# Zero borders from a constant tile, pools that wait by tile, and a first group normalised by channel pairs, in a two-layer convolution kernel

## The chip, the cores and the metric

The kernel runs on one core of a Trainium2 chip. The metric is the device time of one execution in microseconds (us). The engines are called by their names: TensorE (PE in the profile; its weight loads are PEld), VectorE (DVE), ScalarE (ACT), GpSimd (POOL) and SyncE (SP). SP does nothing here but issue DMAs; ScalarE issues some too.

## What is computed

The input x is 32 images of 8 channels, 256 by 256, float32. Two layers follow, each with a residual:

```python
# layer 0
n = gn(x)                                   # GroupNorm: 4 groups of 2 channels
grid = n
for _ in range(15):                         # a coupled map lattice, depthwise 3x3
    mapped = 3.9 * grid * (1 - grid)
    grid = 0.85 * (0.7 * mapped + 0.3 * conv3x3(mapped, K_local)) + 0.15 * n
cml = clip(grid, 1e-4, 1 - 1e-4)
nca = sigmoid(conv1x1(relu(conv3x3(n, Wp) + bp), Wu) + bu)      # 128 hidden channels
g = sigmoid(conv1x1(relu(conv3x3(concat(n, cml, nca), Wg1) + bg1), Wg2) + bg2)
x = x + g * cml + (1 - g) * nca
# layer 1: quantised 3x3 convolution of gn(x), 8 to 8 channels, plus bias
x = x + conv_q(gn(x), weight) + bias
```

All 3x3 convolutions are padded by one zero on each side.

## The kernel before

Intermediate results lie in DRAM scratch tensors: `xp_s` (the normalised image split into a high part hi and a rest lo, with padded rows), `xq_s` (the normalised image with its columns in four phases, the lattice's input), `cm_s` (the lattice's result), `nc_s` (the nca result) and `y_s` (layer 0's result, one tensor an image). `xp_s`, `xq_s`, `cm_s` and `nc_s` exist 12 times and are used in turn; `y_s` exists 32 times. All but `xq_s` have 268 rows, of which rows 1 to 256 hold the image. Row 0 and rows 257 to 267 are the border and must be zero. They are written once at the start (L195 to L202): a tile `zt` of zeros, 258 wide, is the source of four DMAs for each of the 68 tensors, 272 in all, all issued by ScalarE. That code stands in the block of the pool `prep`, which also holds the raw weights; the pool is closed before layer 0 begins.

Layer 0 (from L257) opens its own pools in the space that `prep` gave back. A tile of such a pool that lies in reused space waits, before its first write, for the users of the space.

The work goes in 8 groups of 4 images (`GB`). Four generators give it:

- `normalise` (L288): for a job, an image and a half of its channels (two pairs of channels), `begin` loads each pair (`xr`, 512 KB, L300) and takes its statistics on VectorE (L305); `scale` and `end` get mean and 1/deviation with two small matmuls (L313, L324); then for each pair VectorE normalises (L331), ScalarE writes `xq` (L336), VectorE writes hi (L342), GpSimd writes lo (L343), and six DMAs on SP store them (L345, L352). `xr` has four buffers; `xq`, hi and lo have one each.
- `lattice` (L376): for each channel c of a group one unit of 15 steps over four images. Its input comes with `load(u)` (36 DMAs) in `d_a` and `d_b`. A step is 36 matmuls (L486) on three column tiles of two streams, and VectorE's work on them (L494, L499). Rows are exchanged between partitions by SBUF-to-SBUF DMAs on SP (`exchange`, L449 and L450). After each tile, `background(3)` issues up to three DMAs of the list `later`: the loads of the next unit and the stores of the last.
- `nca` (L553): the hidden layer (L563), its ReLU on ScalarE (L573) and the 1x1 convolution (L580), from row tiles `im` that SP loads from `xp_s` (L541).
- `gate`: the gate's convolution (L755) and the mix; it loads `nc_s`, `cm_s` and x on SP (`nb`, `cq`, `xb`).

TensorE's order is written by hand: `together` runs the lattice of group g and fills between its steps with nca of group g, gate of group g - 1 and normalise of group g + 1, by weights of time. The other engines' orders are the scheduler's, which may move an instruction ahead of others when its operands allow it. Each queue then runs in order.

The head is special: `prep(0, (0,))` normalises the first half (channels 0 to 3) of group 0's four images; then the lattice of group 0 begins, and the second half, `prep(0, (1,))`, runs as the first filling beside it, ahead of nca:

```python
for _ in prep(0, (0,)):
    pass
...
if g == 0:
    fill, t = chain(prep(0, (1,)), fill), t + 20.0
```

Layer 1 (from L879) reads `y_s` an image at a time, quantises and convolves; its pools wait by tile already.

Of the kernel before, what the change touches and what calls it, by code (L numbers as in the profile page):

```python
# [40 lines left out]
P = 128  # L41
C = 8
# [71 lines left out]
def kernel(  # L114
# [46 lines left out]
    rstd_y = cp.tile([P, B], F32, name="rstd_y")  # L161
    dev_y = cp.tile([P, B], F32, name="dev_y")


# [7 lines left out]
    with tc.tile_pool(name="prep", bufs=1) as pp, tc.tile_pool(name="prep2", bufs=2) as pp2:  # L172
# [20 lines left out]

        zt = pp.tile([P, PW], F32, name="zt")
        G.memset(zt, 0.0)  # L195
        for t, n, w in (
            *((t, 2 * C, PW) for t in xp_s), *((t, C, W) for t in (*cm_s, *nc_s, *y_s))
        ):
            nc.scalar.dma_start(dram_ap(t, 0, [[w, n], [1, w]]), zt[:n, :w])
            for i in range(0, 11, 5):  # L200
                m = min(5, 11 - i) * n
                nc.scalar.dma_start(dram_ap(t, (257 + i) * n * w, [[w, m], [1, w]]), zt[:m, :w])  # L202

# [53 lines left out]
    with ExitStack() as one:  # L257

        one.enter_context(tc.manual_schedule(engines={mybir.EngineType.PE}))
        pool = lambda name, bufs, **kw: one.enter_context(tc.tile_pool(name=name, bufs=bufs, **kw))  # L260
        xp, sp2, gp, bp2, st = pool("xp", 4), pool("sp2", 1), pool("gp", 3), pool("bp2", 2), pool("st", 2)
        imp, hp, wk, wk1, np_ = pool("imp", 3), pool("hp", 12), pool("wk", 2), pool("wk1", 1), pool("np", 1)
        ps_c, ps_a = pool("ps_c", 6, space=PSUM), pool("ps_a", 2, space=PSUM)
# [24 lines left out]
        def normalise(jobs):  # L288
# [3 lines left out]

            def begin(b, half):
                xrs = []
                mv = st.tile([P, 2, 2], F32, name="mv", tag="mv")
                stats = st.tile([P, 2, 2, 6], F32, name="stats", tag="stats")
                for i in range(2):
                    g = 2 * half + i
                    xr = xp.tile([P, 2, 2, W], F32, name="xr", tag="xr")
                    nc.sync.dma_start(  # L300
                        xr.rearrange("p c h w -> p (c h) w"),
                        dram_ap(x, (b * C + 2 * g) * H * W, [[W, P], [P * W, 4], [1, W]]),
                    )
                    for j in range(2):
                        V.bn_stats(stats[:, i, j, :], xr[:, j].rearrange("p h w -> p (h w)"))  # L305
                    V.bn_aggr(mv[:, i, :], stats[:, i].rearrange("p j s -> p (j s)"))
                    xrs.append(xr)
                return b, half, xrs, mv

            def scale(b, half, xrs, mv):  # L310
                gs = slice(2 * half, 2 * half + 2)
                pm = ps_c.tile([P, 512], F32, name="pm", tag="pt")
                T.matmul(pm[:, 0:2], avg, mv[:, :, 0], start=True, stop=True)  # L313
                m, rstd = mean_x[:, b, gs], rstd_x[:, b, gs]
                V.tensor_copy(m, pm[:, 0:2])
                e = st.tile([P, 2], F32, name="e", tag="e")
                V.tensor_tensor(e, mv[:, :, 0], m, ALU.subtract)
                V.tensor_tensor(e, e, e, ALU.mult)
                V.tensor_tensor(e, e, mv[:, :, 1], ALU.add)
                return e  # L320

            def end(b, half, xrs, e):
                pv = ps_c.tile([P, 512], F32, name="pv", tag="pt")
                T.matmul(pv[:, 0:2], avg, e, start=True, stop=True)  # L324
                rstd = rstd_x[:, b, 2 * half : 2 * half + 2]
                V.tensor_scalar(rstd, pv[:, 0:2], GN_EPS, None, ALU.add)
                G.tensor_tensor(rstd, rstd, mhalf[:, 0:2], ALU.pow)
                for i, xr in enumerate(xrs):
                    g = 2 * half + i
                    flat = xr.rearrange("p c h w -> p (c h w)")  # L330
# [12 lines left out]
                    G.tensor_tensor(inner(lo), xr, inner(hi).bitcast(F32), ALU.subtract)  # L343
                    for h in range(2):
                        nc.sync.dma_start(  # L345
                            dram_ap(
                                xq_s[b % NBUF], (2 * g * H + P * h) * W, [[W, P], [H * W, 2], [1, W]]
                            ),
                            xq[:, :, h].rearrange("p c q j -> p c (q j)"),
                        )  # L350
                        for j, src in enumerate((hi, lo)):
                            nc.sync.dma_start(  # L352
                                dram_ap(
                                    xp_s[b % NBUF],
                                    (1 + P * h) * ROW + (C * j + 2 * g) * PW,
                                    [[ROW, P], [PW, 2], [1, PW]],
                                ),
                                src.bitcast(F32)[:, :, h, :],
                            )
                    yield 1.0  # L360
                ready.add((b, half))

            ahead = None
            for job in [*jobs, None]:
                now = begin(*job) if job else None
                yield 1.0
                if ahead:
                    e = scale(*ahead)
                    yield 1.0
                    yield from end(*ahead[:3], e)  # L370
                ahead = now

        NG = B // GB
        ready = set()

        def lattice(g):  # L376


            def load(u):


                c, out, dmas = u % C, [], []
                assert all((u // C * GB + i, c // 4) in ready for i in range(GB))
                for s in range(2):
# [57 lines left out]
            def background(n):  # L442
                for _ in range(min(n, len(later))):
                    nc.sync.dma_start(*later.pop(0))

            def exchange(t, k):
# [106 lines left out]
        def nca(b):  # L553
# [80 lines left out]
            im = ahead  # L634
            if (b + 1, 0) in ready and (b + 1, 1) in ready:
                loaded[b + 1] = rows(b + 1, 0, 0)
# [217 lines left out]

        def prep(g, halves):
            return normalise([(b, half) for half in halves for b in range(g * GB, g * GB + GB)])

# [5 lines left out]
        T_NCA, T_GATE, T_PREP, T_LATTICE = 520.0, 340.0, 34.0, 8 * 45 * 1.97  # L863
        for _ in prep(0, (0,)):
            pass
        for g in range(NG):
            fill, t = images(nca, g), T_NCA
            if g:
                fill, t = both(fill, t, images(gate, g - 1), T_GATE), t + T_GATE
            if g + 1 < NG:  # L870
                fill, t = both(fill, t, prep(g + 1, (0, 1)), T_PREP), t + T_PREP
            if g == 0:
                fill, t = chain(prep(0, (1,)), fill), t + 20.0
            together(lattice(g), T_LATTICE, fill, t)
        for _ in images(gate, NG - 1):
            pass
# [113 lines left out]
```

## Time and profile before

| | us |
|---|---|
| three runs | 14463.03, 14468.11, 14472.73 |
| median | 14468.11 |
| the profiled execution | 14447.83 (span of the profile 14446.0) |
| busy: TensorE, VectorE, ScalarE, GpSimd | 13241.2, 8161.7, 4043.5, 2458.8 |
| first statistics of x on VectorE | at 118.3 |
| first dense lattice matmuls | at 217.8 |
| first hidden-layer matmul | at 311.7 |

The mean granted clock of TensorE is 0.959. In the profile's lines L12 is line 12 of the kernel, `out<-in` are the names of tiles or tensors, and "A <- B" in a list of waits says that A sat idle until B was done. The chain of waits follows the work that ended last back from the end, at each step to what released it. Times within a profile are us from its start.

### The profile page before, as it was taken

The numbers are of one execution on the slowest core, as the hardware profiler recorded it, in microseconds if no ns is written. First come the engines' busy times: TensorE is split into PE (matmuls) and PEld (weight loads), VectorE is DVE, ScalarE is ACT, GpSimd is POOL, SyncE is SP. The second block draws the span as 40 slices with busy tenths as digits, with TensorE's granted clock in tenths as the row PEclk, the third lists the DMA queues.
The fourth block names the chain that finished last, engine by engine and source line by source line (L and its number), as shares of the span: only waits on it lengthen the run. The fifth ranks groups of instructions, "written<-read, shape, count | busy, mean of one in ns | idle before, by whom it ended". The sixth has DMA issues, their size and how long they took to land.

```text
span 14446.0 us, 229162 instructions
## 1 busy us (share of the span) xinstructions
PE 13241.2 (92%) x81728; PEld 6420.6 (44%) x81728; DVE 8161.7 (56%) x16290; ACT 4043.5 (28%) x6274; POOL 2458.8 (17%) x4266
## 2 busy tenths in 40 slices
PE   2999999999999999999999999999999999999733
PEld 1554444444444444444444444444444444444211
DVE  3555555555555555555555555555555555555576
ACT  1333223232322232222223222322232222222122
POOL 1110111111111111111111111111111111112300
PEclk9999999999999999999999999999999999999866
DMA  5444444444444444444344434444444433333365
GB/s 149 93 101 93 92 99 105 101 95 104 105 97 101 106 98 98 101 100 111 88 101 105 108 91 102 103 108 94 97 104 108 95 84 80 86 75 79 114 195 176
DMA packets 2259557, 1496.71 MB, mean 104 GB/s; under 512 B 1061248, under 2 KB 2229504, under 8 KB 2258304
## 3 DMA queue, kind: packets, MB, share of 16 engines
q1 hardware_dynamic: 2176976, 1401.95, 41.1%
q10 hardware_dynamic: 81456, 80.12, 1.7%
q8 instruction: 663, 10.86, 0.3%
q14 instruction: 462, 3.78, 0.1%
HBM read 866.48 MB, written 478.69 MB: 93 GB/s over the span
## 4 chain that ended last, share of the span: by engine, by line
PE 76%; DVE 7%; DMA 7%; SPq 4%; issue 3%; ACT 1%; POOL 1%; ACTq 1%; POOLq 0%; DVEq 0%
PE pt L486 34%; PE ph L563 19%; PE pa L755 13%; PE acc L580 7%; DVE gt L494 2%; PE pg L721 1%; DMA im<-xp_s 1%; DMA out_dram<-ob 1%; SPq L941 1%; PE pt L934 1%; DVE m_b L499 1%; DMA yb<-y_s 1%; DMA m_a<-m_a 1%; DMA xb<-in_x_dram 1%; DMA xr<-in_x_dram 1%
## 5 line engine op out<-in xcount | busy, mean ns | idle before, releaser
L486 PE MATMUL pt<-m_a,lw 128*64 128x390 f32 x17280 | 5857.6, 497 | 160.4 <-DMA m_a<-m_a 121.4
L486 PE MATMUL pt<-m_b,lw 128*64 128x384 f32 x17280 | 5825.7, 492 | 23.0 <-DVE m_b L410 17.8
L573 ACT ACTIVATE h<-ph,bp_sb 128x512 f32<-128x512 f32 x4096 | 2584.7, 685 | 6258.0 <-PE ph L563 6187.8
L486 PEld LDWEIGHTS pt<-m_a,lw 128*64 128x64 f32 x17280 | 2312.1, 138 | 1824.9 <-issue 1670.8
L486 PEld LDWEIGHTS pt<-m_b,lw 128*64 128x64 f32 x17280 | 2316.1, 138 | 1601.4 <-issue 1465.6
L563 PE MATMUL ph<-im,wp_hi 48*128 48x512 f32 x12288 | 2713.5, 416 | 104.8 <-DMA im<-xp_s 54.4
L494 DVE SCALAR_TENSOR_TENSOR gt<-pt,d_b 128x390 f32<-128x390 f32 x2880 | 1610.6, 559 | 1828.2 <-PE pt L486 1824.9
L494 DVE SCALAR_TENSOR_TENSOR gt<-pt,d_a 128x384 f32<-128x384 f32 x2880 | 1584.9, 550 | 1826.9 <-PE pt L486 1826.5
L563 PE MATMUL ph<-im,wp_lo 48*128 48x512 f32 x12288 | 2598.5, 399 | 0.0
L503 POOL TENSOR_TENSOR m_b<-m_b,junk 128x12 f32<-128x12 f32 x2688 | 809.2, 301 | 8089.7 <-DVE m_b L499 7597.8
L563 PEld LDWEIGHTS ph<-im,wp_hi 48*128 48x128 f32 x12288 | 1331.4, 188 | 1013.5 <-DVE m_b L499 197.8
L499 DVE SCALAR_TENSOR_TENSOR m_b<-gt 128x390 f32<-128x390 f32 x2688 | 1562.5, 581 | 42.5 <-DVE gt L494 0.9
L499 DVE SCALAR_TENSOR_TENSOR m_a<-gt 128x384 f32<-128x384 f32 x2688 | 1525.9, 568 | 15.6
L563 PEld LDWEIGHTS ph<-im,wp_lo 48*128 48x128 f32 x12288 | 1327.1, 188 | 215.2
L580 PE MATMUL acc<-h,wu_z 128*32 128x512 f32 x8320 | 1170.7, 605 | 12.9 <-ACT h L573 7.3
L755 PE MATMUL pa<-xnb,gw 128*64 128x512 f32 (+1 forms) x3840 | 890.5, 596 | 0.2
L755 PE MATMUL pa<-cmb,gw 128*64 128x512 f32 (+1 forms) x3840 | 852.0, 576 | 10.0 <-POOL cmb L677 10.0
L755 PE MATMUL pa<-nb,gw 128*64 128x512 f32 (+1 forms) x3840 | 849.5, 574 | 0.0
L726 POOL TENSOR_TENSOR d<-cmb,nb 128x512 f32<-128x512 f32 x320 | 511.4, 1598 | 1608.5 <-DVE gate L730 1449.6
L730 DVE TENSOR_TENSOR gate<-gate,d 128x512 f32<-128x512 f32 x320 | 216.0, 675 | 870.3 <-ACT gate L723 856.3
L934 PE MATMUL pt<-qt,qw 128*128 128x512 bf16 (+1 forms) x960 | 269.2, 451 | 477.9 <-ACT ob L935 427.1
L767 ACT ACTIVATE r<-pa,bv 128x512 f32<-128x512 f32 x320 | 213.1, 666 | 1651.3 <-PE pa L755 1650.3
(132 smaller groups left out, 6966.1 us busy)
## 6 DMA issues: line engine op xcount, KB each, us to landing
im<-xp_s SPq DMA_DIRECT2D x1152, 193.5 KB
im<-xp_s SPq DMA_DIRECT2D x1216, 96.8 KB
d_a<-xq_s SPq DMA_DIRECT2D x2048, 36.0 KB
nb<-nc_s SPq DMA_DIRECT2D x288, 256.0 KB
cq<-cm_s SPq DMA_DIRECT2D x288, 256.0 KB
yb<-y_s ACTq DMA_DIRECT2D x29, 2432.0 KB
xb<-in_x_dram SPq DMA_DIRECT2D x544, 128.0 KB
xp_s<-hi SPq DMA_DIRECT2D x256, 258.0 KB
```

What stands on the lines that cost most here:

```text
L486: T.matmul(pt[half], lw[:, c, k, half], beside if part == 2 else own, start=part < 2, stop=part > 0,)
L494: V.scalar_tensor_tensor(gt, pt, FLOOR, d[:, ts, :], ALU.max, ALU.add)
L499: V.scalar_tensor_tensor(to, gt, 1.0, gt, ALU.subtract, ALU.mult)
L503: G.tensor_tensor(edge, edge, junk.unsqueeze(1).to_broadcast([P, 6, 2]), ALU.mult)
L563: T.matmul(ph[:, :n].rearrange("p (h w) -> p h w", w=W), w[64 * i : 64 * i + 48, dx, :], rhs[:, :, dx : dx + W], start=(dx == 0 and w is w ...
L573: S.activation(h[:, :n], ph[:, :n], AF.Relu, bias=bp_sb)
L580: T.matmul(acc[32 * g : 32 * g + 32, :cols], wu_z[:, 24 - 8 * i : 56 - 8 * i], h, start=first, stop=last,)
L726: G.tensor_tensor(three(d), cmb[:, :n, 1 : 1 + W], nin, ALU.subtract)
L730: V.tensor_tensor(y[:, :cols], gt[:, :cols], d[:, :cols], ALU.mult)
L755: T.matmul(three[half], gw[:, s * 3 + dx, half], t[:, :n, dx : dx + W], start=(i == 0), stop=(i == 8),)
L767: S.activation(r1[:, : n * W], pa[:, : n * W], AF.Relu, bias=bv[:, 0:1])
L934: T.matmul(pt, qw[:, dx, :], q[:, k0 : k0 + n, dx : dx + W], start=(dx == 0), stop=(dx == 2))
```

## The change

1. The tile of zeros becomes 64 wide and lies in the pool of constants, which stays open. A border row is written from it as 4 pieces of 64 elements (6 pieces of 43 for the 258 wide rows of `xp_s`). The four DMAs of a tensor are rows 0, 257 to 261, 262 to 266 and 267.
2. ScalarE issues only the first 16 (the borders of the first four `xp_s`). The other 256 wait in a list `borders`. While group 0 runs, `background` takes from it when `later` is empty, up to three DMAs to a call in all, on SP, once the second lattice unit has been set up. What is left after group 0 is issued then.
3. Layer 0's pools wait by tile, and `hp` (12 buffers of the hidden layer's `h`) is placed first.
4. A job of `normalise` is an image and a tuple of channel pairs. For group 0 only pair 0 of the four images is normalised ahead of the lattice; pair 1 of the four, then pairs 2 and 3 of the four, run beside it. The lattice asks for the pair that its channel lies in, nca for all four.
5. The stores of a pair are given out when the next pair begins, and both `xq` stores go first.

```diff
+    zt = cp.tile([P, 64], F32, name="zt")
...
-        zt = pp.tile([P, PW], F32, name="zt")
         G.memset(zt, 0.0)
+        borders = []
         for t, n, w in (
-            *((t, 2 * C, PW) for t in xp_s), *((t, C, W) for t in (*cm_s, *nc_s, *y_s))
+            *((t, 2 * C, PW) for t in xp_s),
+            *((t, C, W) for t in (*nc_s[:GB], *cm_s[:GB], *nc_s[GB:], *cm_s[GB:], *y_s)),
         ):
-            nc.scalar.dma_start(dram_ap(t, 0, [[w, n], [1, w]]), zt[:n, :w])
-            for i in range(0, 11, 5):
-                m = min(5, 11 - i) * n
-                nc.scalar.dma_start(dram_ap(t, (257 + i) * n * w, [[w, m], [1, w]]), zt[:m, :w])
+            k = 64 if w == W else 43
+            for row, m in ((0, 1), (257, 5), (262, 5), (267, 1)):
+                borders.append(
+                    (
+                        dram_ap(t, row * n * w, [[w, m * n], [k, w // k], [1, k]]),
+                        zt[: m * n, :k].unsqueeze(1).to_broadcast([m * n, w // k, k]),
+                    )
+                )
+        for _ in range(4 * GB):
+            nc.scalar.dma_start(*borders.pop(0))
...
-        pool = lambda name, bufs, **kw: one.enter_context(tc.tile_pool(name=name, bufs=bufs, **kw))
-        xp, sp2, gp, bp2, st = pool("xp", 4), pool("sp2", 1), pool("gp", 3), pool("bp2", 2), pool("st", 2)
-        imp, hp, wk, wk1, np_ = pool("imp", 3), pool("hp", 12), pool("wk", 2), pool("wk1", 1), pool("np", 1)
+        pool = lambda name, bufs, **kw: one.enter_context(
+            tc.tile_pool(name=name, bufs=bufs, reuse_waits="tile", **kw)
+        )
+        hp, xp, sp2, gp, bp2 = pool("hp", 12), pool("xp", 4), pool("sp2", 1), pool("gp", 3), pool("bp2", 2)
+        st, imp, wk, wk1, np_ = pool("st", 2), pool("imp", 3), pool("wk", 2), pool("wk1", 1), pool("np", 1)
...
-            def begin(b, half):
+            def begin(b, gs):
...
-                for i, xr in enumerate(xrs):
-                    g = 2 * half + i
+                for g, xr in zip(gs, xrs):
+                    if pending:
+                        stores(*pending.pop())
...
+                    pending.append((b, g, xq))
                     yield 1.0
-                ready.add((b, half))
...
             def background(n):
                 for _ in range(min(n, len(later))):
                     nc.sync.dma_start(*later.pop(0))
+                    n -= 1
+                if g == 0 and units.keys() - {0}:
+                    for _ in range(min(n, len(borders))):
+                        nc.sync.dma_start(*borders.pop(0))
...
-        for _ in prep(0, (0,)):
+        for _ in prep(0, ((0,),)):
             pass
...
             if g == 0:
-                fill, t = chain(prep(0, (1,)), fill), t + 20.0
+                fill, t = chain(prep(0, ((1,), (2, 3))), fill), t + 30.0
             together(lattice(g), T_LATTICE, fill, t)
+            while borders:
+                nc.sync.dma_start(*borders.pop(0))
```

## The prediction

> **What bounds the kernel now.** I read the page first, then the table of windows, then the waits of the SP queue, then the chain of waits over the first 350 us. The page says that TensorE is the bound for nearly the whole run, and that the exceptions are the first slice and the last two:
>
> ```profile
> PE   2999999999999999999999999999999999999733
> ```
>
> The change touches little that TensorE executes, so what it can be worth is TensorE's idle time at the start. The table of windows (columns: stretch, length, busy us of each engine with instructions, granted clock, DMA share, GB/s) gives its size:
>
> ```profile
> 1.00:30.00 29.00, 0.00 (x0) 0.00 (x0) 16.86 (x73) 0.00 (x0) 2.22 (x37) 1.00 0.64 185
> 30.00:112.00 82.00, 0.00 (x0) 0.00 (x0) 2.85 (x15) 0.00 (x0) 0.00 (x0) 1.00 0.23 69
> 118.00:217.00 99.00, 6.04 (x18) 4.22 (x18) 29.45 (x63) 20.21 (x15) 20.21 (x12) 1.00 0.68 189
> 217.00:311.00 94.00, 38.99 (x159) 18.24 (x159) 56.75 (x129) 19.17 (x14) 25.15 (x24) 0.69 0.68 194
> ```
>
> The reader is to see 82 us (30 to 112) in which no engine works and the DMA engines are 23% busy; then 99 us of normalising with TensorE nearly idle; then 94 us in which the lattice runs but TensorE is busy for 39 us. From 311 on TensorE is full. What fills the 82 us stands in the waits of the SP queue (us in total, times, longest) and on ScalarE's queue:
>
> ```profile
> SPq L300 <- DMA y_s<-zt: 93.0, 5, 91.8
> ...
> 112.06 1.05 ACTq L202 DMA_DIRECT2D y_s<-zt  x3
> 114.20 2.06 SPq L300 DMA_DIRECT2D xr<-in_x_dram  x4
> ```
>
> The first load of x waits 91.8 us for the last border store. It reads other memory; it waits because its SBUF tile reuses the space of the pool that held zt. From there the chain of waits (start, us, what) goes pair by pair:
>
> ```profile
> 128.33 2.18 POOL lo L343
> 131.48 3.50 DMA xp_s<-lo
> 135.21 2.18 POOL lo L343
> ...
> 187.82 2.18 POOL lo L343
> 191.47 5.27 DMA xp_s<-lo
> ...
> 217.79 8.52 PE pt L486 x34
> ...
> 300.73 2.18 POOL lo L343
> ...
> 311.65 5.45 PE ph L563 x23
> ```
>
> Each channel pair needs hi and lo, which have one buffer each, so a pair can't start before the stores of the one before it have landed. The eight pairs before the lattice have lo at 128.3 to 187.8: 59.5 / 7 = 8.5 us a pair. The eight under the lattice run from 235.0 to 300.7: 65.7 / 7 = 9.4 us.
>
> **What the Trainium skill says.** "DMA: Bandwidth & Descriptors", section Issuing engines are not separate DMA queues: DMAs from different engines run on the same 16 engines, and moving an issue saves only sequencer time. The trace agrees: from 30 to 112 the limit is ScalarE's issuing at 0.31 us each, with the engines 23% busy. The same page, Specifications, puts the least piece for full rate at 512 B and says that smaller ones are read, changed and written back. The border pieces shrink from 1 KB to 256 B; no row of before shows a 256 B store of zeros, so I bound it below. "TensorE: Matmul & The Clock Gate", Part 1: TensorE starts at half clock and needs about 3.4 us of steady work. The trace agrees: in 217 to 311 the clock is 0.69. This stage stays like that in both kernels, so I take no difference from it.
>
> **The change, part by part.**
>
> *The wait removed.* In the changed kernel as built, SP's order has the four xr loads right after the constants (last at 15.2), each waiting for one earlier DMA only. They issue at about 15.6, where before the first gate's xb loads went (these now stand 2,000 places later in SP's order, still long before group 1 uses them), and land within 4.1 us (114.20 to 118.3), by 22 with some contention. The statistics then stand on VectorE behind the building of the weights up to the reduction at 27.28, which takes 0.23. So they start at 27.5 instead of 118.3: 90.8 us earlier. The other 5.4 us of weight building (27.5 to 32.9) are now mixed with them, ahead of the first rstd. Before, statistics to first lo took 128.3 - 118.3 = 10.0; I add 5 (bounds 1 and 5.4) and get the first lo at 42.5.
>
> *The border stores moved.* ScalarE keeps 16 of the 272; 21 go on SP between the xr loads and the first stores of hi, where SP would wait for some 20 us. At 0.3 to 0.9 us an issue (the row of L202 spans 0.28 to 0.94) they take 6 to 19 us, and each waits for one earlier DMA, at most an xr load: hidden, at worst just. The other 235 go three to a call while group 0 runs, from the 12th of the lattice's exchange steps to the 75th. At 0.31 to 0.55 us they are 73 to 129 us of SP's time. In 311 to 1100 SP has much slack:
>
> ```profile
> SPq L449 <- DVE m_a L499: 166.2, 72, 8.5
> ...
> PE pt L486 <- DMA m_a<-m_a: 49.5, 19, 10.1
> ```
>
> The first line is SP waiting at an exchange for VectorE, and all its waits there sum to 277 us of 789. Queued behind a border store are the exchange itself, the next im loads and the d_a loads; TensorE waits for those. The second line (350 to 1750) is what late exchanges cost now. In packets they are 56 tensors x 12 rows x 8 x 4 = 21,504 of 256 B and some 3,200 of 172 B; 24,700 at 43.6 ns (the page: 41.1% of 16 x 14446 us over 2,176,976 packets) / 16 = 67 us of all engines in some 800 us, 8% of them, or 16% if small pieces cost double, beside the 43% that 350 to 1750 shows: room. From below it costs nothing (the slack covers it), from above 30 us, if waits like the second line's come at each third step, 25 x 1.2 us. No gain is possible in it, since nothing is taken off SP there. I take 8.
>
> *Channel pairs.* Four pairs instead of eight come before the lattice: last lo at 42.5 + 3 x 8.5 = 68.0. From the last lo to the lattice took 217.8 - 187.8 = 30.0 (two rounds of d_a and d_b loads, the same now): 98.0. The twelve others run under the lattice: 217.8 to 235.0 is 17.2 up to the first lo, then 11 x 9.4 = 103.2, then 10.9 from the last lo to the first hidden-layer matmul (300.7 to 311.65): 98.0 + 17.2 + 103.2 + 10.9 = 229.3. That is 82.3 earlier than 311.65. The split itself moves this point by almost nothing, since all 16 pairs still precede it; but TensorE's order as built has six lattice steps before it instead of four, so two steps of 6.02 us (36 matmuls, the chain at 350.69) are already done: 12.0. The four extra small jobs add 4 x 5 small VectorE instructions of 0.15 us and 8 matmuls, 3 us spread over 100; nothing, beside the pair's 9.4.
>
> *Pools that wait by tile, stores one pair later.* SP's and ScalarE's waits at the change to layer 1 (the first loads of yb) are on the same semaphores as before; so nothing there. Later groups' stores are the same DMAs in another order, with TensorE full: nothing.
>
> *The sum*: 82.3 + 12.0 - 8 = 86 us, made against the span of 14446.0 of an execution that took 14447.8. The other runs lie at 14463 to 14473, 0.1% above; I take the 86 off their median: 14468 - 86 = 14382.
>
> **The rivals.**
>
> *The pairs get quicker too*: xr loads no longer run between stores, and both xq stores go ahead of hi and lo, so a pair takes the 6.9 us that the first two took (128.3 to 135.2). Then the lattice starts at 42.5 + 20.7 + 30.0 = 93.2 and the hidden layer at 93.2 + 17.2 + 75.9 + 10.9 = 197: 114 + 12 = 126 with the borders at nothing, 14342. Against it: those two had fresh buffers; the next intervals are 8.4 and 9.8.
>
> *The borders eat half*: 0.7 to 1.1 us of late exchange in each of the 63 steps, 44 to 69 us in place of the 8, gives 14468 - 94 + 44 = 14418 to 14443. For it: the 49.5 us of such waits in group 0, where later groups have 9 to 13 us each; against it: the slack.
>
> *SP becomes the bound in group 0, slower than before*: the exchange of m_a queues behind three border stores at each step. The price is 2.4 us for three at 0.8 us, over 63 steps 151 us: 14468 - 94 + 151 = 14525. It decides from 94 / 63 = 1.5 us a step. For it: SP's timeline, summed in stretches of 100 us of group 0, has 61 to 72 us of issuing in each; against it: the 277 us of slack, twice what the stores take.
>
> *The wait stays in another form*, so that xr doesn't move: 14468. Against it stands the order as built.
>
> **How the numbers follow.** Forecast 0.72, quicker pairs 0.10, half eaten 0.10, SP the bound 0.05, the wait stays 0.03. A measurement of this kernel tells about 0.2%, 29 us, from no change. Forecast, quicker pairs and 0.06 of the half-eaten case are faster by more: 0.88; the rest of that case and the last are within: 0.07; slower 0.05. The forecast's own range: best, first lo at 38.5 and pairs of 8.5 under the lattice give 94.0 + 17.2 + 93.5 + 10.9 = 215.6, so 96 + 12 = 108, 14360; worst, 10.4 a pair (the longest interval in the chain, 252.8 to 263.0, is 10.3) gives 240, so 71 + 12 - 30 = 53, 14415. Half of each neighbouring case in: 14345 to 14425.
>
> **What would show it.** In the profile after: statistics at 27 to 28, first lo near 42, the lattice dense near 98, the first hidden-layer matmul near 229, and no idle stretch on VectorE of more than 20 us. TensorE's waits for m_a in group 0 should be 40 to 80 us; over 130 means the slow rival. Wrong would be a first xr load after 30, or pairs of 12 us.

## The result and the profile after

| | before | after |
|---|---|---|
| median of the four runs on one chip | 14466.45 | 14589.42 |
| lowest to highest | 14463.03 to 14472.73 | 14574.68 to 14612.42 |
| span of the profiled execution | 14446.0 | 14572.9 |
| mean granted clock of TensorE | 0.959 | 0.952 |

The changed kernel is slower: the ratio is 1.0086, with a 95% interval of 1.0068 to 1.0103, some 123 us. The prediction was 14382 us, in 14345 to 14425. It was wrong in direction and in range.

The page's slices of TensorE show that the head did get shorter, and nothing else:

```profile
PE   4999999999999999999999999999999999999733
```

The table of windows of the first 300 us of after (stretch, length, busy us of TensorE, weight loads, VectorE, ScalarE and GpSimd with instructions, clock, DMA share, GB/s):

```profile
0.00:30.00 30.00, 0.00 (x0) 0.00 (x0) 12.36 (x50) 1.28 (x1) 2.17 (x41) 1.00 0.88 155
30.00:60.00 30.00, 4.18 (x16) 3.78 (x16) 20.39 (x75) 3.24 (x2) 4.77 (x6) 1.00 0.81 125
60.00:100.00 40.00, 1.53 (x2) 0.29 (x2) 4.95 (x9) 7.28 (x9) 6.53 (x3) 1.00 0.65 160
100.00:150.00 50.00, 28.04 (x120) 13.02 (x120) 31.16 (x71) 9.03 (x10) 10.21 (x14) 0.83 0.55 140
250.00:300.00 50.00, 45.05 (x279) 23.72 (x279) 23.89 (x49) 14.60 (x23) 3.19 (x10) 0.86 0.47 95
```

The 82 us in which nothing worked are gone: statistics start at 32.6, the last of the four pairs ahead of the lattice has its lo at 79, the lattice runs from 109, and TensorE is full from 255 where it was full from 311. The timeline of the SP queue (start, us, what) shows the xr loads at 19.35 with nothing but constants ahead of them, and what stands right behind them:

```profile
19.35 5.13 SPq L311 DMA_DIRECT2D xr<-in_x_dram  x4
24.58 23.15 SPq L466 DMA_DIRECT2D xp_s<-zt  x21
48.93 0.38 SPq L341 DMA_DIRECT2D xp_s<-hi  x1
```

The chain of waits of after goes through that same place, and then pair by pair:

```profile
23.82 12.74 DMA xr<-in_x_dram
...
44.36 7.44 DMA xp_s<-zt
51.82 7.87 DMA xp_s<-hi
59.78 0.70 DVE hi L375
60.61 2.18 POOL lo L376
...
79.00 2.18 POOL lo L376
...
108.77 8.61 PE pt L508 x34
...
244.41 2.18 POOL lo L376
...
254.94 5.45 PE ph L585 x23
```

To see where the gain went I mark TensorE's progress in the trace by the lattice: it has 34,560 matmuls, 36 a step, 120 steps a group (8 channels of 15 steps). The start of each 15-step unit is a mark that all kernels share. After minus before, in us: at step 15 of group 0 the changed kernel is 69.2 ahead; at step 90 only 9.8; at the start of group 1 13.0 ahead; at the start of group 7 131.6 behind; at the end 127 behind. So there are three findings to explain:

| stretch | before | after | difference |
|---|---|---|---|
| start to step 15 | 436.4 | 367.2 | -69.2 |
| steps 15 to 90 of group 0 | 887.9 | 947.2 | +59.3 |
| groups 1 to 6 (of 1660 us each) | 9959.4 | 10104.0 | +144.6 |

Group 7, beside which no group is normalised, lost nothing (1618.2 before, 1612.3 after). That already points at `normalise`, since everything else in groups 1 to 6 runs in group 7 too. The lists of waits of the stretch of groups 1 to 6 (total us, times, longest), first of before, then of after:

```profile
DVE hi L342 <- DMA xp_s<-hi: 78.1, 24, 7.4
...
PE ph L563 <- DVE gt L494: 23.9, 49, 1.9
```

```profile
DVE hi L375 <- DMA xp_s<-hi: 232.7, 50, 8.4
...
PE ph L585 <- DVE gt L516: 92.6, 92, 3.0
```

VectorE waits three times as long for the stores of hi, and TensorE four times as long for VectorE's `gt`. The first of the two says too much: in before, 40.9 us more in front of hi are put down to other releasers, in after 4.8. All waits in front of hi are 119 us in before and 237 in after, twice as much.

### The profile page after: what moved, and what is told of

Read it like the earlier page. It is cut to its first block, busy times and chain, and to the rows that moved or that the text cites. A ratio compares the mean times of both kernels' runs of the same rounds, so it can differ in the third digit from the quotient of the medians.

```text
span 14572.9 us, 229404 instructions
## 1 busy us (share of the span) xinstructions
PE 13341.4 (92%) x81744; PEld 6457.6 (44%) x81744; DVE 8187.7 (56%) x16310; ACT 4043.2 (28%) x6274; POOL 2454.5 (17%) x4270
## 4 chain that ended last, share of the span: by engine, by line
PE 73%; DMA 8%; DVE 7%; SPq 5%; issue 3%; POOL 1%; ACT 1%; POOLq 0%; DVEq 0%; ACTq 0%
PE pt L508 32%; PE ph L585 18%; PE pa L777 13%; PE acc L602 7%; DVE gt L516 2%; DMA im<-xp_s 2%; PE pg L743 1%; DVE m_b L521 1%; DMA out_dram<-ob 1%; SPq L965 1%; DMA yb<-y_s 1%; SPq L563 1%; PE pt L958 1%; DVE m_a L521 1%; SPq L462 1%
## 5 line engine op out<-in xcount | busy, mean ns | idle before, releaser
L585 PE MATMUL ph<-im,wp_hi 48*128 48x512 f32 x12288 | 2780.5, 421 | 192.6 <-DVE gt L516 99.6
L585 PE MATMUL ph<-im,wp_lo 48*128 48x512 f32 x12288 | 2660.6, 404 | 0.0
L585 PEld LDWEIGHTS ph<-im,wp_hi 48*128 48x128 f32 x12288 | 1384.4, 190 | 1121.6 <-DVE gt L516 276.5
L585 PEld LDWEIGHTS ph<-im,wp_lo 48*128 48x128 f32 x12288 | 1384.6, 191 | 220.1
```

The source lines that it names most:

```text
L585: T.matmul(ph[:, :n].rearrange("p (h w) -> p h w", w=W), w[64 * i : 64 * i + 48, dx, :], rhs[:, :, dx : dx + W], start=(dx == 0 and w is w ...
```

## The experiments

Two theories were set against each other, for the two losses.

- *Late stores* (part 5 of the change): a pair's six stores are issued only when the next pair begins, right ahead of the next hi. Since hi has one buffer, the write of the next hi waits until the stores have read it; VectorE runs in order, so the lattice's `gt` is queued behind that wait, and TensorE behind `gt`.
- *Border stores* (part 2): three border stores to a call of `background` hold SP, and the exchanges of `m_a` and the `im` loads queue behind them.

All kernels compute everything. The ratios are to the kernel before, run on the same chip (its medians on the chips used: 14444.96, 14456.51, 14466.45 and 14476.07); intervals are 95%. The diffs are against the changed kernel unless something else is named.

| kernel | median us | ratio | to step 15 | steps 15 to 90 | groups 1 to 6 |
|---|---|---|---|---|---|
| before | 14466.45 | 1 | 436.4 | 887.9 | 9959.4 |
| after | 14589.42 | 1.0086 (1.0068 to 1.0103) | 367.2 | 947.2 | 10104.0 |
| stores at once | 14405.69 | 0.9974 (0.9964 to 0.9983) | 355.9 | 943.2 | 9945.8 |
| before with late stores | 14564.63 | 1.0086 (1.0069 to 1.0103) | 437.9 | 879.0 | 10070.9 |
| one border a call | 14358.87 | 0.9941 (0.9926 to 0.9956) | 356.2 | 891.2 | 9957.7 |
| no borders in the head | 14414.80 | 0.9978 (0.9970 to 0.9987) | 352.8 | 957.3 | 9949.5 |
| twice the pieces | 14433.18 | 0.9971 (0.9959 to 0.9982) | 359.1 | 949.8 | 9957.4 |
| borders on ScalarE's queue | 14443.99 | 0.9976 (0.9967 to 0.9986) | 418.1 | 893.5 | 9969.0 |
| halves again | 14397.41 | 0.9945 (0.9930 to 0.9960) | 361.6 | 902.5 | 9964.8 |
| one a call, none in the head | 14371.53 | 0.9928 (0.9913 to 0.9942) | 351.0 | 901.2 | 9957.0 |
| three at each third call | 14369.68 | 0.9936 (0.9921 to 0.9951) | 354.9 | 894.0 | 9958.1 |
| stores midway | 14493.01 | 1.0025 (1.0016 to 1.0033) | 360.6 | 943.7 | 10031.0 |
| fewer, larger border stores | 14361.03 | 0.9930 (0.9914 to 0.9947) | 351.9 | 896.7 | 9948.0 |
| whole rows of zeros | 14349.55 | 0.9923 (0.9908 to 0.9937) | 344.8 | 897.5 | 9938.3 |

The last three columns are single executions; groups 1 to 6 of before and of the ten kernels that store at once, where the edits do little or nothing, scatter over 9938 to 9969, so a difference of less than 30 us there says nothing.

### Stores at once: the late stores undone

```diff
                 for g, xr in zip(gs, xrs):
-                    if pending:
-                        stores(*pending.pop())
...
-                    pending.append((b, g, xq))
+                    stores(b, g, xq)
                     yield 1.0
```

> The changed kernel with one part undone: a pair's six stores are given out right behind its hi and lo, not when the next pair begins. Theory A (the late stores): the next pair's hi then finds its buffer free, VectorE no longer stops for 5 to 8 us in the first half of each group, and the 145 us that the changed kernel loses from the start of group 1 to the start of group 7 fall to under 20, with some 20 more back in group 0: about 14420 us, faster than before. Theory B (pools that wait by tile, or the moved buffers, slow every group): the loss a group stays at 20 to 25 us and the time at 14570 or more. Theory C (the border stores on SP are the loss): no more than 10 us move in groups 1 to 6, since no border is stored there.

Measured: 0.9974 in place of 1.0086. The loss of groups 1 to 6 is gone to the last microsecond (9945.8, before 9959.4), and the loss of steps 15 to 90 is nearly untouched (943.2; the 20 us that were expected back in group 0 did not come in this stretch). So this one line of the change costs more than everything else in it brings. Pools that wait by tile, and both `xq` stores first, are kept in this kernel, so neither is the cause. The timelines of VectorE, SP and TensorE show how. First after, where the pair's first hi was written at 3702.7, with the idle time before the instruction in brackets:

```profile
3740.29 0.44 SPq L341 DMA_DIRECT2D xp_s<-hi  x1
3740.83 0.41 SPq L341 DMA_DIRECT2D xp_s<-lo  x1
3741.28 0.50 SPq L341 DMA_DIRECT2D xp_s<-hi  x1
3741.83 0.50 SPq L341 DMA_DIRECT2D xp_s<-lo  x1
...
3747.26 0.69 DVE L375 CAST hi<-xr 128x1024 fp32r<-128x1024 f32 x1 [7.72 <-DMA xp_s<-hi]
3747.87 0.55 DVE L516 SCALAR_TENSOR_TENSOR gt<-pt,d_a 128x384 f32<-128x384 f32 x1
...
3751.31 0.79 PE L585 MATMUL ph<-im,wp_hi 48*128 48x512 f32 x1 [2.35 <-DVE gt L516]
```

Then the same pair with the stores at once:

```profile
3650.70 0.69 DVE L371 CAST hi<-xr 128x1024 fp32r<-128x1024 f32 x1
...
3653.29 0.44 SPq L341 DMA_DIRECT2D xp_s<-hi  x1
3653.82 0.45 SPq L341 DMA_DIRECT2D xp_s<-lo  x1
...
3654.32 0.69 SPq L341 DMA_DIRECT2D xp_s<-hi  x1
...
3655.06 0.73 SPq L341 DMA_DIRECT2D xp_s<-lo  x1
...
3660.61 0.69 DVE L371 CAST hi<-xr 128x1024 fp32r<-128x1024 f32 x1 [1.35 <-DMA xp_s<-hi]
```

The stores take as long in both, some 6 us from the last issue of hi to the release. At once, that time runs while VectorE does other work, and 1.35 us of it is left to wait for. Late, the data lie ready in hi for 37 us, the stores go out at the end of that, and VectorE stands still for 7.72 us with the lattice's `gt` queued behind it; the last line of after shows TensorE idle for 2.35 us until a `gt`.

The second pair of a job has little room in both kernels: its hi comes 4 to 10 us after the last store of the first was issued. The first pair of a job is the difference. In the eight jobs from 3460 to 4900 us of stores at once, its hi comes 134 us or more after the last store of the hi before it was issued; in six of the eight jobs of after it comes 5 to 20 us after.

### Before with late stores: the late stores alone

To the kernel before, only part 5 of the change is added (stores one pair late, both `xq` stores first):

```diff
                     V.tensor_copy(inner(hi), xr)
                     G.tensor_tensor(inner(lo), xr, inner(hi).bitcast(F32), ALU.subtract)
-                    for h in range(2):
-                        nc.sync.dma_start(...)
+                    pending.append((b, g, xq))
                     yield 1.0
```

> The kernel before with only the late stores added (both xq stores first, given out when the next pair begins); borders, pools and halves as before. Theory A: each of groups 1 to 6 loses 20 to 25 us and group 0 about as much: 14467 + 165 = some 14630 us, 1.1% slower. Theories B and C: 14467 within 0.2%.

Measured: 1.0086, where 1.1% was expected. Groups 1 to 6 take 10070.9, 111.5 more than before; group 0 loses nothing in steps 15 to 90 (879.0). So late stores suffice for the loss of the later groups, and they are not the cause of the loss in group 0. In the same stretch of groups 1 to 6 the two waits stand as in after; first this kernel, then stores at once:

```profile
DVE hi L365 <- DMA xp_s<-hi: 220.4, 50, 7.7
...
PE ph L571 <- DVE gt L502: 85.0, 88, 2.9
```

```profile
DVE hi L371 <- DMA xp_s<-hi: 118.6, 40, 7.7
...
PE ph L580 <- DVE gt L511: 27.4, 48, 3.4
```

(All waits in front of hi are 127 us in stores at once, and 119 in before.)

TensorE's wait for `gt` grows from 24 to 93 us from before to after, which is half of the 145. The other half is speed. In groups 1 to 6 of after TensorE's busy time is 9764.5 us in 10104.0, of before 9685.1 in 9959.4: 65 us more idle and 79 us more busy, for the same matmuls (some 60,580). The trace's records of the granted clock hold two values, full and half. Stretches at half clock that begin in groups 1 to 6 sum to 505 us in after, 461 in before with late stores, 365 in before and 335 in stores at once. By estimate, 140 us more at half clock are at most 70 us of lost work, near the 79 us of busy time.

The Trainium skill ("TensorE: Matmul & The Clock Gate", Part 1) says that after an idle window of about 3.4 us the array falls back to half clock, and must be busy for about as long to get it back. The traces agree with that in part. The half-clock stretches can be sorted by the longest idle time of TensorE, as the trace has it, that ends within 5 us ahead of them or runs into them:

| half-clock stretches of groups 1 to 6 | before | stores at once | before with late stores | after |
|---|---|---|---|---|
| behind an idle time over 3.4 us | 31 (259 us) | 32 (253 us) | 31 (256 us) | 31 (249 us) |
| behind shorter ones alone | 17 (106 us) | 14 (82 us) | 33 (205 us) | 40 (256 us) |

The whole growth is in the second row, where no idle time is longer than 3.3 us; 28 of after's 71 stretches begin within 7 us after a wait for `gt`, 7 of before's 48. So the added half clock goes with the short waits for `gt`, though none of them lasts longer than 3.0 us, less than the page's window. How much idle time it takes, these runs don't show.

### One border a call, and at each third call three

Against stores at once. The list of borders is taken from one at a time, all through the kernel, so that steps 15 to 90 see 84 of them and not 223:

```diff
-                if g == 0 and units.keys() - {0}:
-                    for _ in range(min(n, len(borders))):
-                        nc.sync.dma_start(*borders.pop(0))
+                if n > 0 and borders and units.keys() - {0}:
+                    nc.sync.dma_start(*borders.pop(0))
...
-            while borders:
-                nc.sync.dma_start(*borders.pop(0))
```

> As e1_stores_now, and the background gives out one border store to a call instead of up to three, in every group and not in group 0 alone. If bursts of border stores on SP delay the exchanges and image loads, the time between lattice step 15 and step 90 gets shorter by 20 to 40 us, and the whole by as much less a little that is paid in group 1: about 14395. If what group 0 loses is only the late stores, this equals e1_stores_now within 10 us.

Measured: 0.9941, and 891.2 us for steps 15 to 90 (before: 887.9), more than the 20 to 40 us that were expected. The border stores of that stretch are what cost group 0 its 52 us. The tables of zt's tile in this stretch (line, queue, operation, count: least, median and longest ns, first and last start), of stores at once and of one border a call:

```profile
L461 SPq DMA_DIRECT2D y_s<-zt x128: 652/765/1227, 715.0 to 1180.4; - x128
L461 SPq DMA_DIRECT2D cm_s<-zt x48: 654/776/914, 440.5 to 709.9; - x48
L461 SPq DMA_DIRECT2D nc_s<-zt x47: 660/765/904, 408.9 to 621.2; - x47
```

```profile
L460 SPq DMA_DIRECT2D nc_s<-zt x48: 677/779/1258, 532.3 to 1206.9; - x48
L460 SPq DMA_DIRECT2D cm_s<-zt x25: 667/722/847, 759.4 to 1238.8; - x25
L460 SPq DMA_DIRECT2D xp_s<-zt x11: 594/622/632, 496.5 to 529.4; - x11
```

One store holds SP for 0.765 us; 223 of them hold it for 167.8 us in a stretch of 943, and SP's issuing, summed from its timeline, goes from 556 us of 888 (63%) before to 730 of 943 (77%). With one a call it is 626 of 891 (70%). In TensorE's lists of waits of the stretch the exchange and the `im` loads stand first in both; stores at once, then one border a call:

```profile
PE pt L503 <- DMA m_a<-m_a: 34.1, 19, 5.1
PE ph L580 <- DMA im<-xp_s: 17.4, 14, 2.0
```

```profile
PE ph L579 <- DMA im<-xp_s: 19.2, 12, 5.4
PE pt L502 <- DMA m_a<-m_a: 14.0, 11, 3.1
```

Of the 52 us, 31 are idle time of TensorE, 20 of these waits of the lattice for the exchange, and 21 are more busy time, with half clock for 92 us in place of 61.

Is it the burst of three that hurts, or the amount? The same rate, in bursts (against one border a call):

```diff
                 if n > 0 and borders and units.keys() - {0}:
-                    nc.sync.dma_start(*borders.pop(0))
+                    turn.append(1)
+                    if len(turn) % 3 == 0:
+                        for _ in range(min(3, len(borders))):
+                            nc.sync.dma_start(*borders.pop(0))
```

> As e3_one_border, with the same rate of border stores in bursts: three at every third call that has room. If the burst is what delays an exchange, step 15 to step 90 grows from 891 towards 920 and the time by 20 to 40 us over e3_one_border (ratio to before 0.996 to 0.997 instead of 0.994). If only the number of stores in group 0 counts, it equals e3_one_border within 10 us (0.9935 to 0.995).

Measured: 894.0 us for the stretch and a ratio of 0.9936 (one a call: 891.2 and 0.9941). Bursts of three and single stores cost the same. It is the amount in the stretch that decides; whether of stores, of bytes or of SP's time, the next section tells apart.

### Twice the pieces, and whole rows: what makes a store long

Why is a border store 0.765 us, where the old ones took 0.31? Either the number of pieces or their pattern. Against stores at once, the 256 wide rows from pieces of 32 elements, so 8 in place of 4:

```diff
-            k = 64 if w == W else 43
+            k = 32 if w == W else 43
```

> As e1_stores_now, with the 256 wide border rows written as 8 pieces of 32 elements instead of 4 of 64. In e1_stores_now a border store holds SP for 0.75 us, where a 1 KB row piece held ScalarE's queue for 0.31. If that time comes from the number of pieces, a store of these tensors takes about 1.2 us, lattice step 15 to step 90 grows from 943 by 40 to 60 us and the whole to some 14450. If a store's issue costs the same whatever its pieces, nothing moves: 14406 within 10.

Measured: no difference. The ratio is 0.9971, the stretch 949.8, and the store's issue as long as with 4 pieces:

```profile
L461 SPq DMA_DIRECT2D y_s<-zt x128: 654/764/1192, 727.1 to 1186.4; - x128
```

So neither twice the packets nor half their size shows in this stretch. Then, against stores at once, whole rows from a wide tile, in the constants' pool as in the change but without the repeat (`hp` gives up one of its 12 buffers for the room):

```diff
-    zt = cp.tile([P, 64], F32, name="zt")
+    zt = cp.tile([P, PW], F32, name="zt")
...
-                        dram_ap(t, row * n * w, [[w, m * n], [k, w // k], [1, k]]),
-                        zt[: m * n, :k].unsqueeze(1).to_broadcast([m * n, w // k, k]),
+                        dram_ap(t, row * n * w, [[w, m * n], [1, w]]),
+                        zt[: m * n, :w],
...
-        hp, ... = pool("hp", 12), ...
+        hp, ... = pool("hp", 11), ...
```

> As e1_stores_now, with a zero tile of full width, so that a border row is one piece with no repeated source; to make room hp has 11 buffers instead of 12. If the repeated source makes the issue long, a store takes 0.31 to 0.45 us on SP as in the kernel before, the 168 us of issuing in step 15 to 90 fall to 70 to 100, and that stretch falls from 943 to 900 to 920. If 0.75 us is what SP takes for any store of these, nothing moves. Groups 2 to 6 show what the lost buffer of hp costs.

Measured: 0.9923 (0.9908 to 0.9937), the lowest ratio here (the intervals of the one-border kernels overlap it), though still with three borders to a call. The lost buffer of `hp` costs nothing that shows (9938.3 for groups 1 to 6). In steps 15 to 90 there are 204 border stores now, and they take 71 us:

```profile
L460 SPq DMA_DIRECT2D y_s<-zt x128: 263/312/727, 682.7 to 1123.2; - x128
L460 SPq DMA_DIRECT2D cm_s<-zt x44: 263/301/698, 418.8 to 675.2; - x44
L460 SPq DMA_DIRECT2D nc_s<-zt x32: 288/322/804, 493.8 to 599.6; - x32
```

The stretch takes 897.5: the loss of 55 us against before has become 10. Two kernels that leave about as much border issuing in the stretch, one 63 us with 84 stores of 0.75 us, one 71 us with 204 of 0.35, come out within 6 us of each other, and that is the second sign that SP's time is the cause and not the number or the bytes of the stores. The tile of 64 columns is thus what made part 2 dear: the pattern in repeated pieces costs 0.45 us more an issue. (It has a dimension more on both sides, and a repeat in the source; which of these it is, the runs don't separate. The stores of hi above, with three dimensions on both sides and no repeat, took 0.44 to 0.69. The 258 wide rows in pieces of 43 took 0.60, and 0.42 as whole rows, so the extra time isn't one number.)

In this kernel the head is 11 us shorter as well; of that below.

### Borders on ScalarE's queue: an edit that did something else

Against stores at once, the background's border stores are issued by ScalarE:

```diff
-                        nc.sync.dma_start(*borders.pop(0))
+                        nc.scalar.dma_start(*borders.pop(0))
```

> As e1_stores_now, with the background's border stores issued by ScalarE instead of SP. If their cost is SP's issue time ahead of exchanges and image loads, step 15 to step 90 falls from 943 to 890 to 905 us and the whole to about 14365; if it is traffic on the DMA engines or the read and write back of small pieces, it stays at 943; if ScalarE is hurt instead (the ReLU of the hidden layer waits behind three issues of 0.75 us), it rises over 960.

Measured: 0.9976, but not for the reason it was made for. ScalarE's order is the scheduler's, and it put the border stores ahead of group 0: they run from 24 to 303 us, and step 15 starts at 418.1 and not 355.9. What it says of ScalarE as the place for background stores is therefore nothing. Two things can still be read. Steps 15 to 90, now free of borders, take 893.5 us, as the theory of the border stores asks. And the store is as long on this queue (the table of zt's tile):

```profile
L461 ACTq DMA_DIRECT2D y_s<-zt x128: 685/779/1362, 158.5 to 302.7; - x128
```

So the 0.77 us do not belong to SP: the pattern takes as long on ScalarE's queue.

### No borders in the head

Against stores at once; the tile of zeros is rewritten from a tile of the lattice just ahead of the first background border, so that the scheduler can't put 21 of the stores ahead of the first pair:

```diff
                 if g == 0 and units.keys() - {0}:
+                    if not late:
+                        late.append(1)
+                        V.tensor_scalar(zt, d_a[0][:, 0, :], 0.0, None, ALU.mult)
                     for _ in range(min(n, len(borders))):
```

> As e1_stores_now, and the tile of zeros is written anew from the lattice's first input before the background uses it, so that no border store of the background can stand ahead of the first pairs' stores (21 did). If those 21 delayed the head, the second hi comes 7 to 8 us earlier (near 52 instead of 59.8), the lattice starts near 100 instead of 108.8 and the time is 8 to 12 us under e1_stores_now. If the head is bound by the loads of x, nothing moves.

Measured: the second hi at 50.3 and not 56.2, the lattice dense at 94.8 and not 104.1, so the 21 stores did cost some 9 us at that point. By step 15 it is 3.1 us (352.8 against 355.9). Steps 15 to 90 then take 957.3 against 943.2, with 226 border stores against 223; all of these 14 us are busy time of TensorE, with half clock for 120 us against 92, and why isn't settled. The ratio, 0.9978 against 0.9974, shows no gain. Together with one border a call the ratio is 0.9928, the stretch 901.2:

> e3_one_border and e4_late_borders together: one border store to a call, none of them ahead of the first pairs' stores. The head should be that of e4_late_borders (second hi near 50, lattice dense near 96, first hidden-layer matmul some 10 us earlier than in e3_one_border), and group 0 that of e3_one_border: about 14349. If the head's gain is given back in group 0, as it was in e4_late_borders, it equals e3_one_border, 14359.

Measured against one border a call alone (0.9941): the intervals overlap, so nothing more than 0.3% can be said; step 15 starts 5.2 us earlier. Whole rows shorten the head more simply: the 32 stores that stand there take 0.42 us each (median), the second hi comes at 47.4, and step 15 starts at 344.8.

On top of one a call, none in the head, rows 257 to 267 of a 256 wide tensor go in one store, so that four stores of a tensor become two:

```diff
-            for row, m in ((0, 1), (257, 5), (262, 5), (267, 1)):
+            for row, m in ((0, 1), (257, 11)) if w == W else ((0, 1), (257, 5), (262, 5), (267, 1)):
```

> As e8_one_late, with rows 257 to 267 of the 56 tensors that are 256 wide written by one DMA instead of three (88 partitions): 160 border stores in all instead of 272. If the cost goes with the number of issues at 0.75 us, 84 us of SP's time go away, groups 0 and 1 get shorter by 5 to 15 us and the ratio to before is some 0.992. If the last of the border stores' cost is already hidden, it stays at 0.993.

Measured: 0.9930 against 0.9928, nothing. With one store a call there are as many stores in the stretch as before (93, 70.5 us), they only end earlier.

### Halves again: the channel pairs undone

Against one border a call, two pairs an image ahead of the lattice, as before the change:

```diff
-        for _ in prep(0, ((0,),)):
+        for _ in prep(0, ((0, 1),)):
...
-                fill, t = chain(prep(0, ((1,), (2, 3))), fill), t + 30.0
+                fill, t = chain(prep(0, ((2, 3),)), fill), t + 20.0
```

> As e3_one_border, with group 0 normalised by halves as in the kernel before: eight pairs ahead of the lattice, eight beside it. The prediction gave the split 12 us (two lattice steps more beside the normalising). On that, the first hidden-layer matmul stays within 10 us of e3_one_border and the time is some 10 to 15 us longer, about 14371. If the split is worth the four pairs that it moves behind the lattice's start, 35 us or more, about 14395.

Measured: 0.9945 against 0.9941, not to be told apart by the times. In the trace the lattice is dense at 144.5 and not 104.8, but step 15 starts at 361.6 and not 356.2, and step 90 at 1264.1 and not 1247.4. The pairs are worth some 5 to 17 us: the size of the 12 that the prediction gave them, but single executions with this scatter don't prove it.

### Stores midway

Against the changed kernel, the stores go out half a gap after the pair, in place of a whole one:

```diff
-                    pending.append((b, g, xq))
-                    yield 1.0
+                    yield 0.5
+                    stores(b, g, xq)
+                    yield 0.5
```

> The changed kernel with a pair's stores given out halfway between the pair and the next one. If what costs is that VectorE's hi waits for stores issued just ahead of it, half a gap (some 25 us in groups 1 to 6) is enough for them to land: groups 1 to 6 take 1653 to 1665 us each as in e1_stores_now, the ratio to before is about 0.9975. If lateness itself costs (a later xp_s or xq_s, another order on SP), half of the loss stays: groups of some 1670, ratio about 1.002.

Measured: 1.0025 (1.0016 to 1.0033), groups 1 to 6 10031.0: half of the loss. That half a gap would suffice is wrong. The list of waits of groups 1 to 6 shows fewer but longer ones:

```profile
DVE hi L371 <- DMA xp_s<-hi: 167.5, 20, 10.8
...
PE ph L581 <- DVE gt L512: 39.8, 52, 3.2
```

The 20 waits are of 8.4 us in the mean. Half a gap by TensorE's order is not half a gap on SP and VectorE: of the hi in the stretch from 3650 to 4870 us, a job's second comes 18 to 43 us after its first, but only 5 to 9 us after the last store of it was issued. Why VectorE then stands idle in some of these (gaps of 18, 21 and 43 us) and has other work in the rest (23 to 38 us) isn't settled. The kernel's TensorE waits sum to only 16 us more for `gt` than in before; of its 72 us of groups 1 to 6, 51 are idle time, spread over many waits, and 20 busy time.

## Why the prediction was wrong

**The step that decided: stores one pair later.** The prediction put it as "the same DMAs in another order, with TensorE full: nothing". Measured alone it costs 0.86%, and in the changed kernel its removal takes 1.12% back (1.0086 to 0.9974, 162 us against the runs of before on each chip). The reasoning failed in two places that the profile of before showed. TensorE "full" isn't TensorE without waits: there was a row of 44.5 us of hidden-layer matmuls waiting for `gt` in the whole run. And the profile of before had VectorE waiting for the stores of hi, 145.6 us in all. The prediction even named that hi has one buffer and that a pair can't begin before the stores of the one before have landed, and used it for the head only. In the steady state the stores were issued right behind lo and had, at every second pair, the long gap between two jobs to land. The edit takes that gap away and puts the store's time into VectorE's queue, ahead of the lattice's work.

That the late stores cost more in the changed kernel (1.12%) than alone (0.86%) is left open: the intervals, some 0.85 to 1.39% and 0.69 to 1.03%, overlap.

**The border stores: a term of the right kind, seven times too small.** The sum had 73 to 129 us of SP time and 8 us of cost, with a bound of 30. The issue is 0.765 us and not 0.31 to 0.55, so the SP time is 168 us, and steps 15 to 90 lost 59 us. The durations were taken from the old border stores, whose pattern has no repeat. The slack that was to hold them was there: SP's waits for `m_a`, its largest, fell from 165.6 us in that stretch to 100.1 in after:

```profile
SPq L471 <- DVE m_a L521: 100.1, 40, 6.7
```

All of SP's time without an issue fell from 332 us to 225. So of the 166 us more of issuing 107 went into slack and 59 made the stretch longer, with 225 us of slack left over. The cost isn't in proportion: 62 to 70 us more of issuing (whole rows, one a call) cost 10 and 3 us, 174 us (stores at once) cost 55. So besides the price of a store, setting slack in total against issuing in total failed: room was left, and TensorE waited longer for exchanges and `im` loads all the same.

The case "the borders eat half", 44 to 69 us, had this size right with a chance of 0.10; its mechanism, a late exchange at each step, only in part: of after's 59 us 33 are idle time of TensorE (9 of them waits for the exchange, 17 for `im`), and 26 more busy time. With the store at 0.35 us, inside the range that was assumed, the stretch loses 10 us, close to the assumed 8.

**The rival that had the sign had another mechanism.** "SP the bound in group 0", 14525, asked for waits for `m_a` of over 130 us in group 0. TensorE's list of after from 300 to 1750 has

```profile
PE pt L508 <- DMA m_a<-m_a: 59.9, 27, 8.4
```

within the 40 to 80 that were forecast. Group 0 as a whole is still 13 us ahead at its end. The slowdown comes from the six groups that the prediction had passed over in a sentence.

**The wait removed: right.** The first load of x at 19.35 and not 15.6, statistics at 32.6 and not 27.5 (before: 118.3), first lo at 44.2 (42.5 was forecast).

**The pairs and the 21 stores on SP: about 25 us too good.** The lattice is dense at 108.8 and not 98.0, the hidden layer's first run comes at 254.9 and not 229.3. (One matmul of it stands alone earlier, at 246.0; in before too, at 301.1, where the table of before has the run at 311.7 as the first.) The 21 stores held SP's queue for 23.15 us, waits for earlier DMAs among them, where 6 to 19 were taken as hidden; the first stores of hi stood behind them, and the second hi came at 59.8. Under the lattice a pair took (244.4 - 123.7) / 11 = 11.0 us and not 9.4; with stores at once it is (232.9 - 118.6) / 11 = 10.4. So the head gave 69 us at step 15 of the forecast 94.

**The sum, put together again.** In the kernel with whole rows and stores at once, step 15 starts 91.6 us earlier than in before (the prediction: 94), steps 15 to 90 lose 9.6 (the prediction: 8), and group 1 starts 85.8 us earlier (the prediction: 86). That kernel runs at 14349.55, 107 us under the 14456.51 of before on its chip (interval 91 to 133 from the ratio), more than the 86; groups 1 to 6 are 21 us shorter in its trace, which is inside the scatter. The forecast was thus near for a kernel that keeps the old place of a pair's stores and the old pattern of the border stores; the changed kernel did neither. Part of the match is luck: there the lattice is dense at 93.3, 4.7 us ahead of the forecast, and a pair under it takes (223.3 - 107.3) / 11 = 10.5 us and not 9.4, so that the hidden layer's first run starts at 234.2 and not 229.3.

## What to carry to other kernels

Before a store is moved away from its producer, ask when the source's buffer is written next and by which in-order engine: with a single buffer, the store's time to land is hidden only in the gap between issue and that write. A DMA's price on its issuing queue must be read from a row of the same pattern. And waits on a queue that feeds the bound engine are not all room: here SP issued for 63% of the stretch, 70 us more cost next to nothing, and the 100 us beyond that cost some 50, though 213 us without an issue were left. And a line such as "TensorE full: nothing" should be tested against the list of waits in the stretch it speaks of.

## What the runs showed of the hardware

- Issuing a DMA from SP or ScalarE took 0.31 us (median) for rows of 256 elements from a plain tile, and 0.765 (SP) or 0.78 us (ScalarE) where the row is made of repeats of a short one. Whether it is made of 4 or 8 repeats made no difference (0.765 and 0.764).
- The Trainium skill ("DMA: Bandwidth & Descriptors", Issuing engines are not separate DMA queues) says that issuing from several engines saves only the sequencer's time, "which is usually small relative to the DMA itself". No run here compares an issue with its own transfer, but the sum of the issues was the cost: with 223 of them, 168 us of SP's time, the stretch took 55 us more than in before, with 84, 63 us, it took 3 more, while twice as many and half as large pieces took nothing that could be measured.
- Idle times of TensorE of at most 3.1 us were followed by half clock: 40 such stretches, 256 us, in six groups of after, and 17, 106 us, in before. Over these groups after has 65 us more idle and 79 us more busy time of TensorE for the same matmuls.
